# Depthwise taps in sums of 1024, gates on GpSimd and a new order of the half steps in layer 2

## The chip, the cores and the metric

The kernel runs on one core of a Trainium2 chip. A core has TensorE (PE in the profile), VectorE (DVE), ScalarE (ACT), GpSimd (POOL), and SyncE (SP), which here only issues DMAs. Each engine takes its own instructions in order; semaphores hold an instruction until what it needs is there. The metric is the device time of one execution in microseconds, the median of the runs. All data are fp32.

## The reference

Four layers follow each other on x of shape (2, 64, 256, 256), each of the form x + layer(group_norm(x)). Layer 0 is a dilated 3x3 attention, layer 1 two selective scans, layer 3 a blockwise cosine transform with rounding. The change is in layer 2 alone, which is this, cut to what matters:

```python
x = jnp.einsum('bchw,oc->bohw', x, w_in)            # 64 -> 384 channels
xf = jnp.fft.rfft2(patches_8x8(x)) * fft_filter      # one filter per hidden channel
x = unpatch(jnp.fft.irfft2(xf, s=(8, 8)))
x = lax.conv_general_dilated(x, w_dw, padding=[(1, 1), (1, 1)], feature_group_count=384)  # 3x3 depthwise
x1, x2 = jnp.split(x, 2, axis=1)
x = jax.nn.gelu(x1, approximate=False) * x2          # gate x value, 192 channels
return jnp.einsum('bchw,oc->bohw', x, w_out)         # 192 -> 64 channels
```

## The kernel before

Layer 2 goes down the picture in 32 strips of 8 rows. The 384 hidden channels of the two pictures fill six blocks of 128 partitions: a0, a1, a2 are the gates (x1), b0, b1, b2 the values (x2). Blocks 0 and 1 hold 128 channels of one picture each, block 2 the remaining 64 of both.

The work of a strip has a front and a back. The front makes the filtered image of a strip. `norm` (ScalarE) normalizes, `turn` and `fourier` (TensorE, ScalarE) transpose and transform, `hidden` (L915, TensorE) makes the 384 hidden channels in two PSUM tiles `f`, `scaled` (L922, VectorE) multiplies each of the two by the filter into `gf`, `image` (L941, TensorE) transforms back into a PSUM tile `pz`, and ScalarE copies that into the image `z` (L949). There are two `f` tiles and two `pz` tiles in PSUM. Three tiles `z` hold a strip: (a1, a2), (a0, b2), (b1, b0). `edges` (L957, L959, GpSimd) copies the last two rows of a strip to the head of the next and clears the side columns.

The back computes the 3x3 depthwise convolution as nine taps a block, for the strip that the front has finished, in two halves of four rows (1024 elements a partition):

- Values: VectorE, one multiply (L978) and eight multiply-adds (L981) into a PSUM tile `acc`, each on two rows (512 elements), so the two row pairs of a half take turns. Then VectorE multiplies the sum by the gate (L1039, `value_dve`). For b2 of the first half, `value_late` writes the sum to SBUF and GpSimd multiplies (L1047).
- Gates a1 and a2: ScalarE multiplies by the tap (L1016, into one of three `prod` buffers), GpSimd adds (L1020, `gate_pool`); ScalarE applies the gelu (L994) when `flush` is called, three operations into the next sum or in half step 14.
- Gate a0: TensorE multiplies by a diagonal matrix nine times into the PSUM tile `pcv` (L1062, `gate_pe`), and ScalarE applies the gelu from there (L1070).

`project` (L1091, L1098, TensorE) contracts the gated values `gl` of two rows to the output channels, and `finish` (L1109, L1110, VectorE) adds the input, takes statistics for the next normalization, and stores. The PSUM tile `po2`, which transposition, Fourier transform and projection share, has one buffer.

The order is written out by hand. The loop over `u` makes eight steps a strip, each with two half steps (`g`), so a strip has 16 half steps `i`; the back runs nine steps behind the front. `quota(n, i, parts)` deals a list of n operations evenly over the half steps. In each half step, in the program's order: TensorE's `hidden`; up to four of VectorE's taps (`soon`); the two filter products; a projection or output where due; then four places `n`, each with an image, one of TensorE's tap steps, and ScalarE's and GpSimd's share; then the rest of VectorE's taps. TensorE's 36 tap steps go four to a half step, so they fill the first nine; the operations of `gate_pool` fill fourteen. GpSimd's b2 gate is in half step 5; `flush` and `edges` are in half step 14.

VectorE's list of a strip is b2 (late), b0, b1 in the first half and b0, b2, b1 in the second; GpSimd's is a2, a1, a2, a1. A `gl` tile of 1024 elements is drawn from seven buffers, six for the gated blocks and one for the late value.

Of the kernel before, what the change touches and what calls it, by code (L numbers as in the profile page):

```python
# [120 lines left out]
class Kernel:  # L121
# [695 lines left out]
    def layer2(self, x, y, coeffs):  # L817
        nc, tc, a = self.nc, self.tc, self.a
# [14 lines left out]
        nstrip = H // 8  # L833
        with ExitStack() as ctx:
# [5 lines left out]
            with tc.tile_pool(name="l2w", bufs=1) as pool, tc.tile_pool(  # L840
                name="l2wp", bufs=1, space=PSUM
# [5 lines left out]
            taps = {}  # L847
# [17 lines left out]
            pool = ctx.enter_context(tc.tile_pool(name="l2", bufs=2))  # L865
# [1 line left out]
            p_f = ctx.enter_context(tc.tile_pool(name="l2pf", bufs=2, space=PSUM))  # L867
            p_z = ctx.enter_context(tc.tile_pool(name="l2pz", bufs=2, space=PSUM))
            p_c = ctx.enter_context(tc.tile_pool(name="l2pc", bufs=1, space=PSUM))
            p_a = ctx.enter_context(tc.tile_pool(name="l2pa", bufs=2, space=PSUM))  # L870
            p_o = ctx.enter_context(tc.tile_pool(name="l2po", bufs=1, space=PSUM))

            x_half, x_T, x_f, gf, z, gl, xres = {}, {}, {}, {}, {}, {}, {}
# [42 lines left out]
                    ph.append(p)  # L916
                return ph

            def scaled(t, g, ph):
                for b in range(2):  # L920
                    o = pool.tile([P, 2 * HID], F32, name="gf", bufs=8)
                    nc.vector.tensor_tensor(o, feff, ph[b], ALU.mult)  # L922
                    gf[t, g, b] = o
# [45 lines left out]
            def taps_of(s, name, m0, r, last):  # L969


                acc, ops = {}, []

                def step(k, m, n):
                    w, src = taps[name][:, k : k + 1], near(s, name, m0 + m, n, k)
                    if k == 0:
                        acc[m] = p_a.tile([P, 2, W], F32, name="acc")[:, :n]
                        nc.vector.tensor_scalar(acc[m], src, w, None, ALU.mult)  # L978
                        return
                    out = last(m, n) if k == 8 and last else acc[m]  # L980
                    nc.vector.scalar_tensor_tensor(out, src, w, acc[m], ALU.mult, ALU.add)  # L981

                for k in range(9):
                    for m in range(0, r, 2):
                        ops.append(lambda k=k, m=m: step(k, m, min(2, r - m)))
                return ops, acc

            def new_gl(s, h, i, r):
                t = pool.tile([P, 4, W], F32, name="gl", bufs=7)
                gl[s, h, i] = t  # L990
                return t[:, :r]

            def gelu(t):
                nc.scalar.activation(t, t, AF.Gelu)  # L994
# [31 lines left out]
                        out.append(lambda m=m, k=k: step(m, min(2, r - m), k))  # L1026
                return out

            def gate_dve(s, h, i, r):
                t = new_gl(s, h, i, r)  # L1030
                ops, _ = taps_of(s, f"a{i}", 4 * h, r, lambda m, n: t[:, m : m + n])
                return ops + [lambda: gelu(t)]

            def value_dve(s, h, i, r=4):
                ops, acc = taps_of(s, f"b{i}", 4 * h, r, None)

                def gate(m, n):
                    t = gl[s, h, i][:, m : m + n]
                    nc.vector.tensor_tensor(t, t, acc[m], ALU.mult)  # L1039

                return ops + [lambda m=m: gate(m, min(2, r - m)) for m in range(0, r, 2)]

            def value_late(s, h, i):

                t = pool.tile([P, 4, W], F32, name="gl", bufs=7)
                ops, _ = taps_of(s, f"b{i}", 4 * h, 4, lambda m, n: t[:, m : m + n])
                return ops, lambda: nc.gpsimd.tensor_tensor(  # L1047
                    gl[s, h, i], gl[s, h, i], t, ALU.mult
                )

            def gate_pe(s, h, i, r=4):
# [62 lines left out]
            def quota(n, i, parts):  # L1114
                return n * (i + 1) // parts - n * i // parts

            E = mybir.EngineType
            with tc.manual_schedule(engines={E.PE, E.DVE, E.Activation, E.Pool, E.SP}):
# [9 lines left out]
                for u in range(n_u + 12):  # L1128
# [2 lines left out]
                    v = u - 9  # L1131
                    s, j = divmod(v, 8)
                    if j == 0 and 0 <= s < nstrip:
                        dve, gate_late = value_late(s, 0, 2)
                        for h, i in ((0, 0), (0, 1), (1, 0), (1, 2), (1, 1)):
                            dve += value_dve(s, h, i)
                        pe = gate_pe(s, 0, 0) + gate_pe(s, 1, 0)
                        gps = []
                        for h, i in ((0, 2), (0, 1), (1, 2), (1, 1)):
                            gps += gate_pool(s, h, i)  # L1140
                        n_dve, n_gps = len(dve), len(gps)
                    if front:
                        if u % 4 == 2 and u // 4 + 2 < 2 * nstrip:
# [14 lines left out]
                    for g in range(2):  # L1158
                        i = 2 * j + g
                        left = quota(n_dve, i, 16) if 0 <= v and dve else 0  # L1160
                        if front:
                            ph = hidden(t, 2 * odd + g)
                        soon = min(4, left)
                        for _ in range(soon):
                            dve.pop(0)()
                        if front:
                            scaled(t, 2 * odd + g, ph)
                        if out and g == 1 and not odd:
                            finish(*out, po)
                        if out and g == odd:  # L1170
                            po = project(*out)
                        images = ((0, 1), (2,))[g] if 0 < u <= n_u else ()
                        n_pe = min(4, len(pe))
                        if i == 5 and 0 <= s < nstrip:
                            gate_late()
                        for n in range(4):
                            if n < len(images):
                                image(u - 1, images[n])
                            if n < n_pe:
# [139 lines left out]
```

## Time and profile before

| What | us |
|---|---|
| median of 3 runs (lowest, highest) | 19522.35 (19519.64, 19525.44) |
| profiled execution | 19522.79, span 19521.0 |
| layer 2, from its first input to its last output | 15734 to 19197 |
| 31 strips with input, first vector tap to last | 15798 to 19072, 3274 in all |
| busy in these 3274: PE, DVE, ACT, POOL | 2944.9, 3014.1, 2265.7, 2690.5 |

A row of the page's groups reads: line, engine, operation, output <- inputs, shapes, count; behind the bar the time busy in us and the mean of one in ns; then the idle time of that engine just before the group's instructions, and what ended it. A row of a timeline has the start in us, the length, the engine and line, the operation, and in brackets the wait just before it. Two instructions of one engine can overlap by their fill and drain, so the distance between starts says more than the length. The mean granted clock of TensorE is 0.92 of full speed in the 3274 us.

### The profile page before, as it was taken

How to read it: one execution, taken by the hardware profiler on the slowest of the kernel's cores; microseconds unless marked ns; L12 is line 12 of the kernel's file. 1: busy time of each engine (PE TensorE's matmuls, PEld its weight loads, DVE VectorE, ACT ScalarE, POOL GpSimd, SP SyncE). 2: the span in 40 equal slices, each digit the busy share in tenths (PEclk: the TensorE clock that was granted, in tenths of full speed). 3: DMA queues.
4: the chain of work that ended last, by engine and by line, in shares of the span. 5: the costliest groups of instructions: out<-in, count | busy, mean ns of one | idle time of the engine just before them, and what ended most of it. 6: DMA issues, size and time to landing. Idle time of an engine off the chain costs nothing. (4 is left out here: it accounts for less than half of the span.)

```text
span 19521.0 us, 166010 instructions
## 1 busy us (share of the span) xinstructions
PE 14578.1 (75%) x48720; PEld 4850.7 (25%) x48720; DVE 18176.5 (93%) x17790; ACT 12176.5 (62%) x17418; POOL 16771.1 (86%) x8614
## 2 busy tenths in 40 slices
PE   7996767777767777677677677676777689899896
PEld 3441111111111111111111111111111145545454
DVE  6888999999999999999999999999999979999997
ACT  2225666666666666666666666666666656666664
POOL 5997888888888888888888888888888868888885
PEclk9996666666666666666666666666666689999998
DMA  3116666666666666666666666666666611000104
GB/s 122 56 51 151 151 156 148 155 150 151 155 148 155 152 151 153 149 156 153 150 151 151 156 152 151 151 151 157 150 154 150 149 34 32 30 30 30 32 29 146
DMA packets 662208, 2439.06 MB, mean 125 GB/s; under 512 B 131888, under 2 KB 201264, under 8 KB 450160
## 3 DMA queue, kind: packets, MB, share of 16 engines
q1 hardware_dynamic: 661296, 2428.43, 51.9%
q8 instruction: 385, 6.31, 0.1%
q14 instruction: 527, 4.32, 0.1%
HBM read 1990.14 MB, written 437.78 MB: 124 GB/s over the span
## 5 line engine op out<-in xcount | busy, mean ns | idle before, releaser
L792 DVE TENSOR_TENSOR_SCAN h<-da,st,h 128x512 f32<-128x512 f32 x8192 | 9837.5, 1262 | 310.6 <-ACT da L789 226.0
L796 POOL TENSOR_TENSOR h<-h,cb 128x2048 f32<-128x2048 f32 x2048 | 9252.4, 4518 | 164.8 <-DMA d_dv<-du 0.2
L789 ACT ACTIVATE da<-dl,p_a 128x512 f32<-128x512 f32 x8192 | 5564.1, 688 | 3976.2 <-DVE h L792 3884.0
L561 PE MATMUL py<-h,t_c_quad 128*32 128x512 f32 x16384 | 3252.2, 817 | 1646.5 <-POOL h L796 1645.6
L561 PE MATMUL pb<-bc,t_c_sel 64*128 64x512 f32 x3072 | 2697.0, 972 | 2385.8 <-DVE h L773 2380.4
L773 DVE TENSOR_TENSOR h<-dv,pb 128x2048 f32<-128x2048 f32 x1536 | 3470.8, 2260 | 41.0 <-DMA dv<-d_dv 41.0
L1020 POOL TENSOR_TENSOR gl<-gl,prod 128x512 f32<-128x512 f32 x2056 | 2606.7, 1271 | 658.5 <-ACT prod L1016 545.2
L755 POOL TENSOR_TENSOR h<-dv,cb 128x2048 f32<-128x2048 f32 x512 | 2318.7, 4529 | 16.7 <-DMA dl<-d_dl 16.7
L981 DVE SCALAR_TENSOR_TENSOR acc<-z,tap_b,acc 128x512 f32<-128x512 f32 (+1 forms) x3032 | 2046.7, 746 | 1.0
L561 PEld LDWEIGHTS pb<-bc,t_c_sel 64*128 64x128 f32 x3072 | 661.7, 267 | 4411.3 <-DVE h L773 4347.8
L795 POOL COPY st<-h 128x4 f32<-128x4 f32 x2048 | 383.7, 187 | 1362.9 <-DVE h L792 1331.9
L1016 ACT ACTIVATE prod<-z,tap_a 128x512 f32<-128x512 f32 x2056 | 1410.4, 715 | 194.8 <-POOL gl L1020 190.5
L561 PEld LDWEIGHTS py<-h,t_c_quad 128*32 128x32 f32 x16384 | 423.5, 122 | 3812.4 <-POOL h L796 3221.0
L561 PE MATMUL mm<-xin,p_conv 64*128 64x512 f32 x4096 | 1318.5, 773 | 15.7 <-DMA x1t<-y 15.7
L1062 PE MATMUL pcv<-z,diag 128*128 128x512 f32 x2322 | 1142.9, 616 | 44.7 <-ACT gl L1070 41.4
L941 PE MATMUL pz<-t_c_inv,gf 128*128 128x128 f32 (+1 forms) x8192 | 1013.4, 304 | 5.7 <-ACT z L949 4.3
L941 PEld LDWEIGHTS pz<-t_c_inv,gf 128*128 128x128 f32 (+1 forms) x8192 | 822.7, 177 | 488.4 <-issue 310.8
L561 PE MATMUL mm<-u,p_dt 128*128 128x512 f32 x1024 | 929.1, 1061 | 0.0
L561 PE MATMUL py<-u,p_d 128*128 128x512 f32 x1024 | 820.9, 894 | 0.0
L949 ACT COPY z<-pz 128x512 f32<-128x512 f32 x768 | 453.1, 594 | 548.7 <-PE pz L941 494.3
L922 DVE TENSOR_TENSOR gf<-feff,f 128x384 f32<-128x384 f32 x1024 | 518.1, 547 | 218.7 <-PE f L915 218.7
L561 PEld LDWEIGHTS mm<-xin,p_conv 64*128 64x128 f32 x4096 | 459.7, 244 | 981.2 <-issue 981.1
(169 smaller groups left out, 17321.9 us busy)
## 6 DMA issues: line engine op xcount, KB each, us to landing
cb<-d_bc SPq DMA_DIRECT2D x2048, 320.0 KB
dl<-d_dl SPq DMA_DIRECT2D x2048, 256.0 KB
dv<-d_dv SPq DMA_DIRECT2D x2048, 256.0 KB
d_dl<-delta SPq DMA_DIRECT2D x256, 512.0 KB
d_dv<-du SPq DMA_DIRECT2D x256, 512.0 KB
xin<-in_x SPq DMA_DIRECT2D x16, 2048.0 KB
xt<-in_x SPq DMA_DIRECT2D x32, 1024.0 KB
y<-yt SPq DMA_DIRECT2D x128, 256.0 KB
```

The lines of the kernel that those rows point to most:

```text
L561: nc.tensor.matmul(out, lhsT, rhs, start=start, stop=stop)
L755: nc.gpsimd.tensor_tensor(h, t["dv", b], t["cb", b][:, 0].unsqueeze(1).to_broadcast([P, 4, T]), ALU.mult,)
L773: nc.vector.tensor_tensor(h, t["dv", b], pb.unsqueeze(1).to_broadcast([P, 4, T]), ALU.mult)
L789: nc.scalar.activation(da, t["dl", b][:, k], AF.Exp, scale=ws[m]["a"][:, k, j : j + 1])
L792: nc.vector.tensor_tensor_scan(h[:, k], da, h[:, k], state[m, b][:, j, k : k + 1], ALU.mult, ALU.add)
L796: nc.gpsimd.tensor_tensor(h, h, t["cb", b][:, 1 + j].unsqueeze(1).to_broadcast([P, 4, T]), ALU.mult)
L922: nc.vector.tensor_tensor(o, feff, ph[b], ALU.mult)
L941: nc.tensor.matmul(pz[i * n : (i + 1) * n, k, :, 16 * g : 16 * g + 16], gf[t, 2 * e + g, b][:, c0 : c0 + n], inv, start=True, stop=True,)
L981: nc.vector.scalar_tensor_tensor(out, src, w, acc[m], ALU.mult, ALU.add)
L1016: nc.scalar.activation(prod, near(s, name, 4 * h + m, n, k), AF.Copy, scale=w)
L1020: nc.gpsimd.tensor_add(acc, acc, prod)
L1062: nc.tensor.matmul(box["t"], diag[:, k], near(s, f"a{i}", 4 * h + m, n, k), start=k == 0, stop=k == 8,)
```

## The change

1. *Taps of 1024 in one sum.* `taps_of` works on all four rows of a half at once, in a PSUM tile `acc` of 1024 elements with one buffer (before: two of 512). The gates of `value_dve` take 1024 elements, too.
2. *Order of the values.* VectorE's list is b2 (late), b1, b0 in both halves; GpSimd's is a1, a2 in both. GpSimd multiplies b2 in both halves, in half step 8 and in half step 14, the latter between `flush` and `edges`. The value has its own SBUF tile `value` with one buffer, and `gl` six.
3. *TensorE's taps.* `quota` deals the 36 steps over fourteen half steps, two or three in each.
4. *Filter pairs apart.* Two taps stand before the first filter product, and one is put between the two products.

```diff
-            p_a = ctx.enter_context(tc.tile_pool(name="l2pa", bufs=2, space=PSUM))
+            p_a = ctx.enter_context(tc.tile_pool(name="l2pa", bufs=1, space=PSUM))
...
-            def scaled(t, g, ph):
+            def scaled(t, g, ph, between):
                 for b in range(2):
+                    if b:
+                        between()
                     o = pool.tile([P, 2 * HID], F32, name="gf", bufs=8)
                     nc.vector.tensor_tensor(o, feff, ph[b], ALU.mult)
                     gf[t, g, b] = o
...
+            def taps_of(eng, s, name, m0, r, first, last):
+                box = {}
+                def step(k):
+                    w = taps[name][:, k : k + 1]
                     if k == 0:
+                        box["t"] = first()
+                        eng.tensor_scalar(box["t"], near(s, name, m0, r, 0), w, None, ALU.mult)
                         return
+                    out = last(box["t"]) if k == 8 else box["t"]
+                    eng.scalar_tensor_tensor(
+                        out, near(s, name, m0, r, k), w, box["t"], ALU.mult, ALU.add
+                    )
+                return [lambda k=k: step(k) for k in range(9)], box
...
+            def new_acc(r):
+                return p_a.tile([P, 4, W], F32, name="acc")[:, :r]
...
             def value_late(s, h, i):
-                t = pool.tile([P, 4, W], F32, name="gl", bufs=7)
-                ops, _ = taps_of(s, f"b{i}", 4 * h, 4, lambda m, n: t[:, m : m + n])
+                box = {}
+                def last(_):
+                    box["v"] = pool.tile([P, 4, W], F32, name="value", bufs=1)
+                    return box["v"]
+                ops, _ = taps_of(nc.vector, s, f"b{i}", 4 * h, 4, lambda: new_acc(4), last)
                 return ops, lambda: nc.gpsimd.tensor_tensor(
-                    gl[s, h, i], gl[s, h, i], t, ALU.mult
+                    gl[s, h, i], gl[s, h, i], box["v"], ALU.mult
                 )
...
-                        dve, gate_late = value_late(s, 0, 2)
-                        for h, i in ((0, 0), (0, 1), (1, 0), (1, 2), (1, 1)):
-                            dve += value_dve(s, h, i)
+                        dve, gps, gates = [], [], []
+                        for h in range(2):
+                            ops, late_gate = value_late(s, h, 2)
+                            gates.append(late_gate)
+                            dve += ops + value_dve(s, h, 1) + value_dve(s, h, 0)
+                            gps += gate_pool(s, h, 1) + gate_pool(s, h, 2)
                         pe = gate_pe(s, 0, 0) + gate_pe(s, 1, 0)
-                        gps = []
-                        for h, i in ((0, 2), (0, 1), (1, 2), (1, 1)):
-                            gps += gate_pool(s, h, i)
...
-                        soon = min(4, left)
+                        soon = min(2, left)
                         for _ in range(soon):
                             dve.pop(0)()
                         if front:
-                            scaled(t, 2 * odd + g, ph)
+                            more = left > soon
+                            scaled(t, 2 * odd + g, ph, lambda: dve.pop(0)() if more else None)
+                            soon += more
...
-                        n_pe = min(4, len(pe))
-                        if i == 5 and 0 <= s < nstrip:
-                            gate_late()
+                        taps_pe = quota(n_pe, i, 14) if i < 14 and 0 <= v and pe else 0
+                        if i == 8 and 0 <= s < nstrip:
+                            gates.pop(0)()
...
                         if i == 14:
                             flush()
                             if 0 <= s < nstrip:
+                                gates.pop(0)()
                                 if s + 1 == nstrip:
                                     frame(nstrip)
                                 edges(s + 1)
```

More of the change, by code (lines that the diff above doesn't have):

```diff
@@ L967, in near @@
                 return z[s, p][:, e, m0 + dy : m0 + dy + r, dx : dx + W]
[L969 to L975, printed above, removed]
+            def taps_of(eng, s, name, m0, r, first, last):
+                box = {}
+                def step(k):
+                    w = taps[name][:, k : k + 1]
                     if k == 0:
-                        acc[m] = p_a.tile([P, 2, W], F32, name="acc")[:, :n]
-                        nc.vector.tensor_scalar(acc[m], src, w, None, ALU.mult)
+                        box["t"] = first()
+                        eng.tensor_scalar(box["t"], near(s, name, m0, r, 0), w, None, ALU.mult)
                         return
[L980 to L986, printed above, removed]
+                    out = last(box["t"]) if k == 8 else box["t"]
[3 more added lines that the diff above has]
+                return [lambda k=k: step(k) for k in range(9)], box
             def new_gl(s, h, i, r):
-                t = pool.tile([P, 4, W], F32, name="gl", bufs=7)
+                t = pool.tile([P, 4, W], F32, name="gl", bufs=6)
                 gl[s, h, i] = t
                 return t[:, :r]
+            def new_acc(r):
+                return p_a.tile([P, 4, W], F32, name="acc")[:, :r]
             def gelu(t):
@@ L1027, in gate_pool, with gate_dve, gate @@
                 return out
[L1029 to L1032, printed above, removed]
-            def value_dve(s, h, i, r=4):
[L1035 to L1041, printed above, removed]
-            def value_late(s, h, i):
-                t = pool.tile([P, 4, W], F32, name="gl", bufs=7)
-                ops, _ = taps_of(s, f"b{i}", 4 * h, 4, lambda m, n: t[:, m : m + n])
+            def gate_dve(s, h, i, r=4):
+                ops, box = taps_of(
+                    nc.vector,
+                    s,
+                    f"a{i}",
+                    4 * h,
+                    r,
+                    lambda: new_acc(r),
+                    lambda t: new_gl(s, h, i, r),
+                )
+                return ops[:8] + [lambda: (ops[8](), gelu(gl[s, h, i][:, :r]))]
+            def value_dve(s, h, i, r=4):
+                ops, box = taps_of(
+                    nc.vector, s, f"b{i}", 4 * h, r, lambda: new_acc(r), lambda t: t
+                )
+                def gate():
+                    t = gl[s, h, i][:, :r]
+                    nc.vector.tensor_tensor(t, t, box["t"], ALU.mult)
+                return ops + [gate]
+            def value_late(s, h, i):
+                box = {}
[3 more added lines that the diff above has]
+                ops, _ = taps_of(nc.vector, s, f"b{i}", 4 * h, 4, lambda: new_acc(4), last)
                 return ops, lambda: nc.gpsimd.tensor_tensor(
-                    gl[s, h, i], gl[s, h, i], t, ALU.mult
+                    gl[s, h, i], gl[s, h, i], box["v"], ALU.mult
                 )
@@ L1133, in layer2 @@
                     if j == 0 and 0 <= s < nstrip:
-                        dve, gate_late = value_late(s, 0, 2)
-                        for h, i in ((0, 0), (0, 1), (1, 0), (1, 2), (1, 1)):
-                            dve += value_dve(s, h, i)
+                        dve, gps, gates = [], [], []
[4 more added lines that the diff above has]
+                            gps += gate_pool(s, h, 1) + gate_pool(s, h, 2)
                         pe = gate_pe(s, 0, 0) + gate_pe(s, 1, 0)
-                        gps = []
-                        for h, i in ((0, 2), (0, 1), (1, 2), (1, 1)):
-                            gps += gate_pool(s, h, i)
+                        n_pe = len(pe)
                         n_dve, n_gps = len(dve), len(gps)
@@ L1178, in layer2 @@
                                 image(u - 1, images[n])
-                            if n < n_pe:
+                            if n < taps_pe:
                                 pe.pop(0)()
```

## The prediction

> **What bounds the kernel now.** I began with the slices of the page, to find layer 2.
>
> ```profile
> PE   7996767777767777677677677676777689899896
> DVE  6888999999999999999999999999999979999997
> POOL 5997888888888888888888888888888868888885
> ```
>
> Layers 0, 1 and 3 are untouched; layer 2 is the stretch from about the 33rd slice to the 39th, where no engine is at 100% and three are near it. The first vector tap starts at 15798 us and the last strip without fresh input at 19072 us: 31 strips in 3274 us, **105.6 us a strip**. Sixteen half steps make a strip, so 6.6 us each.
>
> Next, the groups of 27 strips in the middle (16077 to 18935 us). Idle time stands behind the bar.
>
> ```profile
> L981 DVE SCALAR_TENSOR_TENSOR acc<-z,tap_b,acc 128x512 f32<-128x512 f32 x2539 | 1718.7, 748 | 0.0
> L922 DVE TENSOR_TENSOR gf<-feff,f 128x384 f32<-128x384 f32 x864 | 437.0, 546 | 148.4 <-PE f L915 148.4
> L1039 DVE TENSOR_TENSOR gl<-gl,acc 128x512 f32<-128x512 f32 x270 | 179.2, 680 | 73.2 <-ACT gl L994 63.1 <-ACT gl L1070 10.1
> L1020 POOL TENSOR_TENSOR gl<-gl,prod 128x512 f32<-128x512 f32 x1728 | 2194.7, 1273 | 507.0 <-ACT prod L1016 412.1
> L1047 POOL TENSOR_TENSOR gl<-gl 128x1024 f32<-128x1024 f32 x27 | 64.0, 2371 | 0.0
> ```
>
> VectorE waits (148.4 + 73.2 + 3.7 before the statistics) / 27 = 8.3 us a strip: 5.5 for TensorE's `f`, 2.7 for a gelu. GpSimd waits far more. Durations overlap, so I took start-to-start times from the timelines. VectorE:
>
> ```profile
> 16796.71 4.70 DVE L981 SCALAR_TENSOR_TENSOR acc<-z,tap_b,acc 128x512 f32<-128x512 f32 x7
> 16803.66 1.02 DVE L922 TENSOR_TENSOR gf<-feff,f 128x384 f32<-128x384 f32 x2 [2.25 <-PE f L915]
> ...
> 16808.27 0.69 DVE L1039 TENSOR_TENSOR gl<-gl,acc 128x512 f32<-128x512 f32 x1 [2.34 <-ACT gl L994]
> ...
> 19178.79 4.23 DVE L981 SCALAR_TENSOR_TENSOR acc<-z,tap_b,acc 128x256 f32<-128x256 f32 x8
> ```
>
> Seven taps of 512 in a row start 0.659 us apart (4.61/7), 0.089 less than one lasts. They alternate between two sums. The last line is the end of the layer, one sum alone: (4.23 - 0.49)/7 = 0.534 us apart, 0.044 *more* than the 0.490 that one lasts.
> VectorE's strip: 108 taps x 0.659 = 71.2; 10 gates x 0.595 = 6.0; 32 filter products x 0.465 = 14.9; 4 outputs with statistics x 1.32 = 5.3. Sum 97.3, plus 8.3 waited, gives the 105.6.
>
> GpSimd, at the seam of two strips, and in the last strip, where nothing else holds it:
>
> ```profile
> 16844.19 8.02 POOL L1020 TENSOR_TENSOR gl<-gl,prod 128x512 f32<-128x512 f32 x6 [0.27 <-ACT prod L1016]
> 16852.16 1.04 POOL L957 COPY z<-z 128x1032 f32<-128x1032 f32 x1
> ...
> 16861.28 1.27 POOL L1020 TENSOR_TENSOR gl<-gl,prod 128x512 f32<-128x512 f32 x1 [5.55 <-ACT prod L1016]
> ...
> 19135.28 10.60 POOL L1020 TENSOR_TENSOR gl<-gl,prod 128x512 f32<-128x512 f32 x8 [0.19 <-ACT prod L1016]
> 19146.07 10.60 POOL L1020 TENSOR_TENSOR gl<-gl,prod 128x512 f32<-128x512 f32 x8 [0.19 <-ACT prod L1016]
> ```
>
> Unhindered, eight adds take 10.79 us, so its strip is 8 x 10.79 = 86.3, one gate 2.4 and the three border copies 3.5 (16852.16 to about 16855.7): 92.2, and 13.4 us of avoidable waiting.
>
> Last, TensorE in the chain of waits:
>
> ```profile
> 16865.49 3.44 PE pcv L1062 x8
> 16868.93 0.84 PE f L915 x4
> ```
>
> Where it sets the pace it runs `f` in 0.84, twelve `pz` in 1.03, eight in 1.09, a tap step (two matmuls) in 0.86 to 1.06. Four tap steps in each of the first nine half steps give 6.9 us each (16747.65 to about 16810); later half steps have none and TensorE waits up to 4.7 us. So VectorE sets most of a strip, TensorE the first nine half steps, GpSimd one gate.
>
> **What the Trainium skill says.** *VectorE: DVE Perf Modes*, section on the TRN2 errata: a latency is paid per instruction, once for a large tile. The trace agrees: 256 elements take 490 ns, 512 take 748. The same page, "The DRAIN you can't avoid", says a semaphore between vector operations costs nothing extra; the trace disagrees for a sum that waits for itself (0.534 us apart; at the fixed part of the alternating taps, 256 elements would be 0.40). *TensorE: Matmul & The Clock Gate*, Part 1: the clock halves after an idle window and needs a busy one to recover. It agrees: after 3.7 us of waiting, `f` x4 took 2.11 us at 16742, not 0.84. *PSUM — Partial Sum Buffer*, Specifications: a bank holds 512 fp32, so a sum of 1024 spans two. No run here shows a vector write over two.
>
> **The change, part by part** (us per strip).
>
> *Taps of 1024.* 108 taps become 54. By the slope 258 ns per 256 elements one lasts 748 + 516 = 1264 ns: 1.175 apart if nothing holds it, 1.308 after its own predecessor. 54 x 1.175 = 63.5. Gates: the two of b2 in the second half move to GpSimd, the other eight become four of 1024, 678 + 2 x 257 = 1192 ns, 1.11 apart: 4.4. With 14.9 and 5.3 unchanged: 88.1. In the changed order 26 of the 58 taps and gates follow directly on the one that they wait for: 26 x 0.133 = 3.5. **VectorE 91.6**, 5.7 less. Bounds: no such holds 88.1, all held 95.8. The two-bank write I take at full pace because `h<-dv,pb` reads 2048 PSUM elements in 2260 ns; its other bound is in the last rival.
>
> *Filter pairs apart.* A tap between the two products removes no instruction. It lets TensorE refill the first `f` bank one tap earlier and fills a hold; counted above. From the last product to the next first one there are three taps, about 3.7 us, where there were seven of 0.659, 4.6; `f` (0.84) and a transpose (0.44) still fit.
>
> *TensorE's taps over fourteen half steps.* 36 steps as before, now 2 or 3 in each. A strip: `f` 13.4, `pz` 25.2, taps 36 x 0.95 = 34.2, transposes and Fourier 5.4, projections 4 x 2.07 = 8.3: 86.5, of which 81 in the fourteen, 5.8 each. Slow clock at the start of a strip adds about 3 in total, two seams between tap groups (`pcv` has one bank) 1.5. That is 6.1 against GpSimd's 6.3 below, so most of the 5.5 us waited for `f` goes. Half steps with a projection reach 7 to 8 and will still stall something.
>
> *Gate order.* Block b1 waits for its gelu at half step 5; the gelu is issued at half step 4, and GpSimd now makes this gate first. Before, both fell in half step 7. I take its 2.7 us as gone; half a step of slack is what hides it.
>
> *GpSimd gates both b2.* 2.4 more. The second gate stands behind the last gelu (0.7 with its signal) and ahead of the border copies, so all that needs the borders moves back by 3.1: ScalarE's first copy of the new image, VectorE's first tap, TensorE's first tap. **GpSimd**: 86.3 + 4.8 + 0.7 + 3.5 = **95.3** without any wait, above VectorE's 91.6. It becomes the bound.
>
> *What is late next.* The second copy, of a0 and b2, ends 0.7 + 2.4 + 2.2 = 5.3 us after the last add. TensorE's first tap waits for it in order, and behind that stands the second image (2.1 with the tap when warm, about 3.9 cold), its copy 0.5 and the second product 0.7, which the first new add needs: 8.6 to 10.4 after the last add, while GpSimd is free at 6.6. I take 9.1, 2.5 of waiting, and 1.0 for the heavy half steps: **98.8 us a strip**. ScalarE's copies are in the same chain; its own work (2265.7 us busy in the 31 strips, 73 each) leaves room.
>
> *Buffers.* One `value` buffer: VectorE writes it again in half step 10, GpSimd reads it in 8; if GpSimd fell two half steps behind, the gate's 2.4 us would be exposed. Six `gl` buffers for six uses: freed by the projection of half step 5, refilled from 7. No DMA and no item of SP's queue moves; the loads run at 30 GB/s here.
>
> *Ends.* The last strip is GpSimd's already (94 us); its extra gate replaces a vector gate of 0.7, so +2. The single last row is unchanged.
>
> Sum against the profiled execution, 19522.8 us (span 19521.0; the median of the runs is 19522.35, the same): 31 x (105.6 - 98.8) = 211, less 2: **19313**.
>
> **Rivals.** *GpSimd alone.* The seam is hidden by the lead of the others, TensorE stays warm: 95.3 a strip, 31 x 10.3 - 2 = 317, 19205. For: GpSimd ran without a gap in the last strip. Against: the first tap's wait for the border copy.
>
> *VectorE stays the bound.* Its waits only change their names: 91.6 + 8.3 = 99.9, gain 175, 19347; with every tap held 104.1, gain 44, 19478. For: at 16838 to 16857 it ran without a pause while the others waited. Against: the named waits come from TensorE's crowding and the late gate.
>
> *Slower: the gate is simply added to GpSimd's loop.* If its 13.4 us of waiting stay, the strip is 95.3 + 13.4 = 108.7, 31 x 3.1 = 96 more, 19620. It decides from 10.3 us of waiting (105.6 - 95.3); I forecast 3.5. For: borders later by 3.1 delay three engines at once, and a cold TensorE follows. Against: some 6 us of the waiting fell in TensorE's crowded half steps.
>
> *The two-bank sum is not at full pace.* At half pace a tap takes some 2.25, VectorE 150, the whole about 20,900. The change loses from a mean tap of about 1.5 (1.24 forecast). Nothing in the profile speaks for it.
>
> **How the numbers follow.** GpSimd with a seam 0.48, GpSimd alone 0.14, VectorE bound 0.27 (a tenth of it within 0.2%), added gate 0.09, two-bank 0.02. About 0.2%, 39 us, is what a measurement of this kernel can tell from no change. Faster: 0.48 + 0.14 + 0.24 = 0.86; same 0.04; slower 0.10, part of the added-gate case ending near zero. The likeliest case alone spans 19260 to 19370 (97 to 100.5 a strip). The 8-in-10 range takes in GpSimd alone at 19200 and VectorE with most of its taps held at 19450.
>
> **What would show it.** Strips 97 to 100 us apart; GpSimd's adds waiting under 6 us a strip beyond their own pace, most at the seam, behind ScalarE; taps of 1024 lasting 1.26 to 1.28 us, 1.18 apart across a filter product and 1.31 in a run; `gf <- f` waits below 3 us a strip; the b1 gate's 2.3 us wait for a gelu gone; the chain of waits with more GpSimd. It is wrong if `f` waits stay at 5 us, if TensorE waits long for the border copies, or if a tap lasts over 1.4.

## The result and the profile after

The changed kernel takes **19422.36 us** (median of 6 runs, 19418.88 to 19425.37) beside 19521.46 for the kernel before in the same runs (6 runs, 19517.28 to 19525.44): a ratio of 0.9949, 95% interval 0.9936 to 0.9962. That is 99 us faster, where 209 were forecast. The profiled execution of the changed kernel has a span of 19423.1 us.

The slices of the page, PE, DVE and POOL again:

```profile
PE   7996677767777677676677677767777679999996
...
DVE  6888999999999999999999999999999978888896
...
POOL 5997888888888888888888888888888878888885
```

In layer 2, from the 34th slice to the 39th, PE now reads 9 throughout, where 8 and 9 took turns, and DVE reads 8 in five slices where it read 9; POOL stays at 8. The groups of the middle strips (16077 to 18935 us, now some 28 strips), read as before:

```profile
L982 DVE SCALAR_TENSOR_TENSOR acc<-z,tap_b,acc 128x1024 f32<-128x1024 f32 x1286 | 1650.8, 1284 | 17.8
L924 DVE TENSOR_TENSOR gf<-feff,f 128x384 f32<-128x384 f32 x895 | 489.5, 547 | 225.7 <-PE f L915 223.3
L979 DVE TENSOR_SCALAR acc<-z,tap_b 128x1024 f32<-128x1024 f32 x168 | 215.8, 1285 | 42.7 <-POOL z L961 39.8
L1051 DVE TENSOR_TENSOR gl<-gl,acc 128x1024 f32<-128x1024 f32 x112 | 136.3, 1217 | 5.8
```
```profile
L1023 POOL TENSOR_TENSOR gl<-gl,prod 128x512 f32<-128x512 f32 x1785 | 2266.8, 1274 | 343.2 <-ACT prod L1019 244.3
L1064 POOL TENSOR_TENSOR gl<-gl,value 128x1024 f32<-128x1024 f32 x56 | 132.0, 2358 | 20.7 <-ACT gl L997 20.7
```
```profile
L1079 PE MATMUL pcv<-z,diag 128*128 128x512 f32 x2011 | 1072.0, 640 | 132.1 <-ACT gl L1087 126.4 <-POOL z L959 5.8
```

and the last of them before the change:

```profile
L1062 PE MATMUL pcv<-z,diag 128*128 128x512 f32 x1944 | 959.5, 616 | 25.7 <-ACT gl L1070 25.7
```

Line numbers have moved: L981 to L982, L922 to L924, L1039 to L1051, L1020 to L1023, L1047 to L1064, L1062 to L1079. VectorE's wait for `f` was to go; it grew, from 148.4 / 27 = 5.5 to 223.3 / 28 = 8.0 us a strip. The gate's wait for a gelu is gone (5.8 us in all of 28 strips, in short gaps behind its own sum's last tap). VectorE's first tap of a strip waits for the border copy, 39.8 / 28 = 1.4. GpSimd's adds wait 343.2 us where they waited 507.0. TensorE's wait for ScalarE's gelu of `pcv`, 25.7 / 27 = 1.0 us a strip before, is 126.4 / 28 = 4.5.

Where that wait sits is seen in one strip. TensorE, ScalarE, VectorE and GpSimd around half step 10, from the timelines:

```profile
16786.69 1.13 PE L1079 MATMUL pcv<-z,diag 128*128 128x512 f32 x2
16791.33 2.07 PE L1079 MATMUL pcv<-z,diag 128*128 128x512 f32 x2 [3.51 <-ACT gl L1087]
16793.33 1.65 PE L915 MATMUL f<-t_w_inT,xf 64*128 64x384 f32 x4
16794.91 2.07 PE L943 MATMUL pz<-t_c_inv,gf 128*128 128x128 f32 x8
```
```profile
16787.78 0.72 ACT L1019 ACTIVATE prod<-z,tap_a 128x512 f32<-128x512 f32 x1 [0.22 <-POOL gl L1023]
...
16790.68 0.59 ACT L1087 ACTIVATE gl<-pcv 128x512 f32<-128x512 f32 x1
```
```profile
16786.11 2.61 DVE L982 SCALAR_TENSOR_TENSOR acc<-z,tap_b,acc 128x1024 f32<-128x1024 f32 x2
16795.01 0.55 DVE L924 TENSOR_TENSOR gf<-feff,f 128x384 f32<-128x384 f32 x1 [6.30 <-PE f L915]
```
```profile
16786.47 10.57 POOL L1023 TENSOR_TENSOR gl<-gl,prod 128x512 f32<-128x512 f32 x8 [0.18 <-ACT prod L1019]
16798.90 10.63 POOL L1023 TENSOR_TENSOR gl<-gl,prod 128x512 f32<-128x512 f32 x8 [1.85 <-ACT prod L1019]
```

36 tap steps dealt over fourteen half steps put the 27th step, the last of a group of nine, in the second place of half step 10 and the first step of the next group in the third place. `pcv` has one buffer, so that step waits until ScalarE has taken the gelu of the group before. The group is complete at 16787.82 (16786.69 + 1.13). ScalarE, which works in order, has a product (with 0.22 us of waiting for GpSimd ahead of it, 16787.78), a normalization, two copies and another product in front of the gelu and starts it at 16790.68. TensorE has waited 3.51 us when it is done, and what follows runs at half the clock (the granted clock is 0.50 from 16791.30 to 16795.00): the tap step takes 2.07 us for 1.13, `f` 1.65 for 0.92, eight `pz` 2.07 for 1.16. All that stood in TensorE's queue behind one tap: VectorE waits 6.30 us for its `f` (16795.01), and GpSimd loses 1.85 us although it is the engine with most to do. The chain of waits goes the same way, through ScalarE's gelu to TensorE and on to VectorE:

```profile
16790.30 0.48 ACT z L951
16790.79 0.50 ACT gl L1087
...
16791.33 2.07 PE pcv L1079 x2
16793.40 1.63 PE f L915 x4
16795.03 0.06 DVE gf L924
```

The seam of two strips on GpSimd (the second gate, then the first add after the borders), and eight of its adds in the last strip, which run at their own pace as before:

```profile
16820.08 2.35 POOL L1064 TENSOR_TENSOR gl<-gl,value 128x1024 f32<-128x1024 f32 x1 [0.74 <-ACT gl L997]
...
16829.63 1.27 POOL L1023 TENSOR_TENSOR gl<-gl,prod 128x512 f32<-128x512 f32 x1 [3.69 <-ACT prod L1019]
```
```profile
19043.57 10.58 POOL L1023 TENSOR_TENSOR gl<-gl,prod 128x512 f32<-128x512 f32 x8 [0.18 <-ACT prod L1019]
```

The seams are not alike, and TensorE's clock tells them apart. In the changed kernel the first add waits 2.23 us in 12 of the 28 seams of the window, 3.6 to 3.8 in 8 and 4.4 to 5.7 in 8. A short and a long one:

```profile
16930.41 1.27 POOL L1023 TENSOR_TENSOR gl<-gl,prod 128x512 f32<-128x512 f32 x1 [2.23 <-ACT prod L1019]
...
17239.38 1.26 POOL L1023 TENSOR_TENSOR gl<-gl,prod 128x512 f32<-128x512 f32 x1 [5.66 <-ACT prod L1019]
```

From the last add to the next first one, the busy time of each engine and, as the third number from the right, the granted clock of TensorE, for the seam shown above and these two:

```profile
16819.35:16829.63 10.28, 8.12 (x37) 4.60 (x38) 8.92 (x11) 4.02 (x7) 5.69 (x7) 0.83 0.13 42
16921.58:16930.41 8.83, 6.58 (x37) 3.81 (x38) 7.33 (x9) 4.03 (x7) 5.68 (x7) 1.00 0.14 45
17227.12:17239.38 12.26, 9.64 (x39) 5.43 (x38) 11.44 (x13) 4.02 (x7) 5.69 (x8) 0.72 0.12 36
```

So the seam lasts 8.8 us at the full clock, and up to 12.3 with part of it at half. Before the change, too, two lengths take turns: the 5.55 us of waiting at 16861.28 that the prediction shows is a short one. From 16334 us on every second seam is like this:

```profile
17603.63 1.27 POOL L1020 TENSOR_TENSOR gl<-gl,prod 128x512 f32<-128x512 f32 x1 [9.29 <-ACT prod L1016]
```

The mean granted clock of the whole window is 0.92 before the change and 0.96 after it.

I took GpSimd's first and last add of each strip from its timeline in this window. "Strip" is the distance of two first adds, "inside" from the first add to the end of the last, "seam" from there to the next first add. The lower part says where it waited for a product (gaps over 0.25 us in front of an add; 72 operations over fourteen half steps tell the half step; "seam" takes in half step 0), all in us a strip, over whole strips with input. The kernels are those of the next section.

| | before | changed | four taps in nine half steps | whole groups | pairs together | all three mended |
|---|---|---|---|---|---|---|
| strip | 105.86 | 102.40 | 105.82 | 100.62 | 100.90 | 97.66 |
| inside | 94.82 | 92.29 | 94.63 | 90.31 | 91.26 | 91.86 |
| seam | 11.05 | 10.10 | 11.19 | 10.31 | 9.64 | 5.81 |
| waits at the seam | 8.2 | 4.2 | 5.2 | 4.6 | 3.7 | 0 |
| half step 2 | 3.1 | 0.9 | 3.0 | 0.4 | 0.4 | 2.2 |
| half steps 4 to 9 | 3.0 | 0.5 | 2.8 | 0.5 | 0.5 | 0.5 |
| half steps 11 to 13 | 0 | 2.2 | 0 | 0 | 1.6 | 0.7 |
| second gate, for its gelu | no gate | 0.7 | 0.7 | 0.7 | 0.7 | 0 |

The change wins 3.46 us a strip. GpSimd's waits in half steps 2 to 9 fell from 6.1 to 1.4 and at the seam from 8.2 to 4.2; against this stand 2.4 more for the gate, 0.7 of waiting for the gelu ahead of it, and 2.2 us of new waits in half steps 11 to 13.

### The profile page after: what moved, and what is told of

It reads as the page before. It is cut to its first block, busy times and chain, and to the rows that moved or that the text cites. A ratio compares the mean times of both kernels' runs of the same rounds, so it can differ in the third digit from the quotient of the medians.

```text
span 19423.1 us, 164029 instructions
## 1 busy us (share of the span) xinstructions
PE 14534.9 (75%) x48720; PEld 4763.2 (25%) x48720; DVE 17991.3 (93%) x15870; ACT 12151.6 (63%) x17418; POOL 16845.3 (87%) x8646
## 5 line engine op out<-in xcount | busy, mean ns | idle before, releaser
L1023 POOL TENSOR_TENSOR gl<-gl,prod 128x512 f32<-128x512 f32 x2056 | 2606.1, 1272 | 460.9 <-ACT prod L1019 346.7
L982 DVE SCALAR_TENSOR_TENSOR acc<-z,tap_b,acc 128x1024 f32<-128x1024 f32 (+1 forms) x1496 | 1901.6, 1271 | 22.3
L1079 PE MATMUL pcv<-z,diag 128*128 128x512 f32 x2322 | 1236.4, 642 | 179.9 <-ACT gl L1087 166.0
L943 PE MATMUL pz<-t_c_inv,gf 128*128 128x128 f32 (+1 forms) x8192 | 964.7, 293 | 7.6 <-ACT z L951 7.3
L924 DVE TENSOR_TENSOR gf<-feff,f 128x384 f32<-128x384 f32 x1024 | 558.7, 547 | 299.9 <-PE f L915 297.4
```

Source lines behind the costliest of these rows:

```text
L943: nc.tensor.matmul(pz[i * n : (i + 1) * n, k, :, 16 * g : 16 * g + 16], gf[t, 2 * e + g, b][:, c0 : c0 + n], inv, start=True, stop=True,)
L982: eng.scalar_tensor_tensor(out, near(s, name, m0, r, k), w, box["t"], ALU.mult, ALU.add)
L1023: nc.gpsimd.tensor_add(acc, acc, prod)
L1079: nc.tensor.matmul(box["t"], diag[:, k], near(s, f"a{i}", 4 * h + m, n, k), start=k == 0, stop=k == 8,)
```

## The experiments

The kernel before took 19521.93 to 19527.35 us beside these kernels, so their times are set beside each other and beside 19422.36; as it took 19521.46 beside the changed kernel, a difference from the changed kernel may be up to 6 us larger than written, and one between two experiments up to 6 us off either way. Two theories stood at the start. **A**: the missing gain sits in the tap groups that end within a half step (the wait above). **B**: it sits in the second b2 gate ahead of the border copies, which makes everything of the next strip late.

### What won the 99 us

*TensorE's taps four to a half step again, the rest of the change kept.*

```diff
-                        taps_pe = quota(n_pe, i, 14) if i < 14 and 0 <= v and pe else 0
+                        taps_pe = min(4, len(pe))
```

> The changed kernel with TensorE's tap steps four to a half step in the first nine, as before the change; order of the values, both b2 gates on GpSimd, taps of 1024 and filter pairs apart stay. If the spreading is what won the changed kernel's 99 us, they go: 19490 or more. If the order of the values won them and the spreading gave about as much as its tap group seams cost (some 50 us), it stays near the changed kernel: 19390 to 19450. Slower than 19560 if half steps of 6.9 us on TensorE now also delay GpSimd with its extra gate.

19529.69 us, ratio 1.0003 (0.9994 to 1.0011): the whole gain is gone.

```profile
16768.52 1.27 POOL L1023 TENSOR_TENSOR gl<-gl,prod 128x512 f32<-128x512 f32 x1 [2.63 <-ACT prod L1019]
...
16783.41 5.33 POOL L1023 TENSOR_TENSOR gl<-gl,prod 128x512 f32<-128x512 f32 x4 [1.13 <-ACT prod L1019]
16789.89 3.85 POOL L1023 TENSOR_TENSOR gl<-gl,prod 128x512 f32<-128x512 f32 x3 [1.14 <-ACT prod L1019]
```

GpSimd waits again in half steps 2, 4 and 5 (2.63, 1.13, 1.14 us), much as before the change, and the mean granted clock of the window is 0.93. So the spreading is what the changed kernel needs for its gain. How much of it comes through the clock, which goes up with it, no run separates. It also shows that GpSimd's second gate isn't simply added to the strip: with 3.1 us more to do, the strip is as long as before, because the waits fell by about as much. The spreading alone in the old order of the values wasn't tried: there VectorE multiplies b0 by gate a0 before the spread taps would have made it.

*The kernel before with taps of 1024 in one sum, nothing else.* Its `taps_of`, `gate_dve`, `value_dve` and `value_late` are written as in the changed kernel, in the old order:

```diff
-                nc.vector.scalar_tensor_tensor(out, src, w, acc[m], ALU.mult, ALU.add)
+                eng.scalar_tensor_tensor(
+                    out, near(s, name, m0, r, k), w, box["t"], ALU.mult, ALU.add
+                )
...
-                        soon = min(4, left)
+                        soon = min(2, left)
```

> The kernel before with one part of the change alone: taps of 1024 in one sum, order, gates and TensorE's deal as before. Taps 1.19 apart across other work and 1.32 in a run, so VectorE needs some 95.5 us a strip where it needed 97.3. If VectorE's work bounds the kernel before as it is, 2 us a strip, about 19465. If its waits for TensorE's crowded half steps and for the late gelu just grow by what is won, 19515 or more.

19526.77 us, ratio 1.0002 (0.9994 to 1.0011). Nothing is won; the strip is 105.73. The groups of VectorE show where the saved work went:

```profile
L922 DVE TENSOR_TENSOR gf<-feff,f 128x384 f32<-128x384 f32 x865 | 438.0, 547 | 166.6 <-PE f L915 166.6
...
L1049 DVE TENSOR_TENSOR gl<-gl,acc 128x1024 f32<-128x1024 f32 x135 | 164.6, 1219 | 102.6 <-ACT gl L995 64.4 <-ACT gl L1082 32.2 <-ACT prod L1017 0.5
```

The wait for `f` is 166.6 / 27 = 6.2 us a strip, from 5.5, and the gates wait (64.4 + 32.2) / 27 = 3.6 for gelus, from 2.7. In all VectorE waits 263.7 / 27 = 9.77 us a strip for other engines, 221.6 / 27 = 8.21 before. Without these waits its strip is 105.73 - 9.77 = 96.0 us, from 105.86 - 8.21 = 97.7: the 1.7 us of work that it saves stand in the waits.

*The changed kernel with taps of 512 in two alternating sums*, the reverse of it (two `acc` of 512, four taps ahead of the products, two between them):

```diff
-            p_a = ctx.enter_context(tc.tile_pool(name="l2pa", bufs=1, space=PSUM))
+            p_a = ctx.enter_context(tc.tile_pool(name="l2pa", bufs=2, space=PSUM))
...
+                for k in range(9):
+                    for m in range(0, r, 2):
+                        ops.append(lambda k=k, m=m: step(k, m, min(2, r - m)))
```

> The changed kernel with one part undone: taps of 512 in two alternating sums, all else (order, b2 gates on GpSimd, TensorE's deal, a pair of taps between the two filter products) as changed. VectorE needs some 96 us a strip, 4 more than changed and about GpSimd's 95.3. If the changed kernel is bound by GpSimd and the seams, at most 1 us a strip is lost: up to 19460. If VectorE's arrival at the strip's end counts in full, 3 to 4 us a strip: 19515 to 19550, no gain left over the kernel before.

19422.04 us, ratio 0.9949 (0.9934 to 0.9964), the changed kernel's time. VectorE waits less, for `f` 145.7 / 28 = 5.2 us for 8.0 and for the borders 27.5 / 28 = 1.0 for 1.4, and the strip is the same 102.40: some 3 us more of work on VectorE cost nothing. In both orders the larger taps only exchange work for waiting.

### Where the other 110 us are

*Whole groups (A): groups of nine end with half steps 3, 6, 10 and 13.*

```diff
-                        taps_pe = quota(n_pe, i, 14) if i < 14 and 0 <= v and pe else 0
+                        deal = (3, 2, 2, 2, 3, 3, 3, 3, 2, 2, 2, 3, 3, 3)
+                        taps_pe = deal[i] if i < 14 and 0 <= v and pe else 0
```

> TensorE's 36 tap steps are dealt (3,2,2,2,3,3,3,3,2,2,2,3,3,3), so a group of nine always ends with its half step and no group starts in the middle of one. Theory A (the excess over the forecast comes from TensorE standing at the seam of two groups until ScalarE's gelu, which is queued behind products that GpSimd holds): the wait of the filter product for f, 8.0 us a strip in the changed kernel, falls to about 3, GpSimd's gap of 1.85 us in the second half of a strip goes, and since VectorE no longer arrives late at the end of the strip the gap at the seam of two strips shrinks from 10.8 to about 9: some 3.5 us a strip, about 19315 us. Theory B (the excess is the gate ahead of the border copies alone): VectorE waits less for f, but the strip stays within 0.8 us of 102.4, 19400 us or more.

19376.82 us, ratio 0.9923 (0.9907 to 0.9940): 46 us below the changed kernel, between the 19315 of A and the 19400 of B.

```profile
DVE gf L924 <- PE f L915: 114.3, 126, 2.5
...
DVE acc L979 <- POOL z L961: 61.6, 28, 2.5
...
PE pcv L1079 <- POOL z L959: 24.5, 28, 6.0
...
PE pcv L1079 <- ACT gl L1087: 7.1, 16, 0.7
```

The columns are the total, the number of waits and the longest, in us. TensorE's wait for the gelu fell from 126.4 to 7.1 and VectorE's for `f` from 223.3 to 114.3; GpSimd's gap in half step 11 is gone. A is right about this wait and it is worth 1.8 us a strip. At the same time the waits for the border copies grew, VectorE's from 39.8 to 61.6.

*Borders ahead of the gate (B): in half step 14 the second gate comes behind `edges`.*

```diff
-                                gates.pop(0)()
                                 if s + 1 == nstrip:
                                     frame(nstrip)
                                 edges(s + 1)
+                                gates.pop(0)()
```

> In half step 14 the border copies stand ahead of GpSimd's second b2 gate, so the borders no longer wait for the last gelu and the gate (3.1 us). Theory A (TensorE's seam inside the strip makes VectorE late, and that sets the strip seam): borders come earlier, but TensorE's f of the next strip still waits for VectorE's late product, so at most 0.8 us a strip is won, 19395 us or more. Theory B (the borders set the strip seam): 2 to 3 us a strip, 19330 to 19360 us.

19399.52 us, ratio 0.9935 (0.9920 to 0.9950): 23 us below the changed kernel. The wait for `f` stays (228.3), as A says. A allows for it with 19395 or more, and B's 19330 to 19360 isn't reached: the gate's place costs, and is the smaller part.

*Both.*

```diff
+                        deal = (3, 2, 2, 2, 3, 3, 3, 3, 2, 2, 2, 3, 3, 3)
...
                                 edges(s + 1)
+                                gates.pop(0)()
```

> Both edits. If each theory holds a part, the borders begin to matter once VectorE is in time: more than the sum of the two single gains; GpSimd near its floor of 95 to 97 us a strip, 19200 to 19260 us. If only A holds, as the first kernel, about 19315. If only B holds, as the second.

19342.95 us, ratio 0.9906 (0.9891 to 0.9920): 79 us below, a little more than the two alone (46 + 23), but 83 us short of the 19260 that were to come if each theory holds a part. The strip is 99.47.

*The second b2 gate as VectorE's last operation of a strip, none of it on GpSimd.*

```diff
-                return ops, lambda: nc.gpsimd.tensor_tensor(
+                eng = nc.vector if h else nc.gpsimd
+                return ops, lambda: eng.tensor_tensor(
...
+                            if h:
+                                dve.append(late_gate)
...
-                                gates.pop(0)()
```

> The b2 gate of the second half is VectorE's last operation of the strip instead of GpSimd's; all else as in the changed kernel. If GpSimd's load of 95.3 us a strip is the bound (the forecast's step), it loses the gate and the wait for the last gelu, 3.1 us, and the strip falls by 2 to 3 us, 19330 to 19360 us. If the stall at TensorE's seam sets VectorE's arrival (theory A), VectorE gets 1.2 us more and the strip stays within 1 us of 102.4, or grows: 19390 to 19460 us.

19398.93 us, ratio 0.9935 (0.9921 to 0.9950): as much as the borders ahead of the gate (23 us), and not what 2.4 + 0.7 us less work on GpSimd would be worth (96). GpSimd's adds wait 402.8 us for 343.2. GpSimd's own work alone is thus no bound of the changed kernel. But VectorE got 1.5 us more to do in exchange (a gate of 1484 ns), so what GpSimd's 2.4 us cost by themselves this run doesn't show.

*No tap step in half step 0, then three in each.* That takes TensorE's first wait for the borders out of the seam:

```diff
+                        deal = (0, 3, 3, 3, 3, 3, 3, 3, 3, 3, 3, 2, 2, 2)
+                        taps_pe = deal[i] if i < 14 and 0 <= v and pe else 0
```

> As e1_seam, whole groups of nine, but dealt (0,3,3,3,3,3,3,3,3,3,3,2,2,2): no TensorE tap in half step 0, so the second image of a strip no longer stands behind a tap that waits for the border copy and runs at the slow clock. If that chain sets the seam of two strips (the forecast's step on what is late next), GpSimd's first add comes 1.5 to 2 us earlier than in e1_seam, 45 to 60 us in all, about 19325. If VectorE's own first tap, which waits for the same border copy, sets it, nothing is won: 19365 or more.

19415.27 us, ratio 0.9946 (0.9931 to 0.9961): a miss. It is 38 us above whole groups alone, although the seam fell from 10.31 to 7.63 us. The gaps moved into half steps 1 and 2 (1.6 and 2.9 us; inside rose from 90.31 to 94.40).

```profile
DVE gf L924 <- PE f L915: 157.5, 92, 3.2
...
DVE acc L979 <- POOL z L961: 74.0, 27, 3.0
...
PE pcv L1079 <- ACT gl L1087: 37.4, 28, 1.4
```

VectorE's first tap now waits 74.0 / 27 = 2.7 us for the border copies, 61.6 / 28 = 2.2 with whole groups, and its filter products stand behind that tap.

*The same deal and the borders ahead of the gate.*

```diff
+                        deal = (0, 3, 3, 3, 3, 3, 3, 3, 3, 3, 3, 2, 2, 2)
...
                                 edges(s + 1)
+                                gates.pop(0)()
```

> e5_first with the border copies ahead of the second b2 gate. With the three waits gone the strip should come near GpSimd's own 95 to 97 us: 19230 to 19290 us. If TensorE with three tap steps in ten half steps running becomes the bound instead (its half step is then 6.3 us on average), 19330 or more, with VectorE waiting for f.

19298.13 us, ratio 0.9886 (0.9869 to 0.9902), strip 98.19. With the borders early the same deal that lost 38 us now wins 45 against the other one (19342.95): the seam falls from 9.48 to 7.51. So the deal is worth nothing until the borders come early, and its three tap steps in ten half steps running are not by themselves what made the run before slow. It stays 8 us above the 19290 expected.

*That kernel with the second b2 gate on VectorE.*

```diff
+                eng = nc.vector if h else nc.gpsimd
...
+                        deal = (0, 3, 3, 3, 3, 3, 3, 3, 3, 3, 3, 2, 2, 2)
...
-                                gates.pop(0)()
```

> Whole groups of nine for TensorE, none in half step 0, and the second b2 gate of a strip as VectorE's last operation in place of GpSimd's (2.4 us less on GpSimd, 1.1 to 1.2 us more on VectorE, the borders directly behind the last gelu). If GpSimd's own work sets the strip once the tap groups and the borders are mended (19298), it is 31 x 2.4 = 74 us faster still, 19210 to 19245. If VectorE and TensorE set it as much, the products of the next strip come 1.2 us later and nothing or less is won: 19280 to 19335.

19296.76 us, ratio 0.9883 (0.9868 to 0.9898): within 2 us of the kernel with the gate on GpSimd. The seam fell to 6.65, and the inside rose from 90.68 to 91.73 although GpSimd does the same work in it. So here, too, handing the gate to VectorE buys nothing; what GpSimd would gain if no other engine took it over no run shows.

### Filter pairs

*The changed kernel with the two filter products directly behind each other.*

```diff
-                            more = left > soon
-                            scaled(t, 2 * odd + g, ph, lambda: dve.pop(0)() if more else None)
-                            soon += more
+                            scaled(t, 2 * odd + g, ph, lambda: None)
```

> The changed kernel without the tap between the two filter products: they stand directly behind each other again, taps of 1024 and everything else as in the changed kernel. GpSimd and the seams of the strips set the pace: within 25 us of the changed kernel, 19400 to 19450. If VectorE's own pace sets it, each half step holds one more tap behind its own sum (0.13 us) and the first f tile comes free one tap later: 16 x 0.13 = 2.1 us a strip, 65 us, 19485 or more.

19385.16 us, ratio 0.9927 (0.9911 to 0.9944): 37 us *below* the changed kernel, outside both expectations. Setting the pairs apart costs. What it does to `f` is seen at a seam; TensorE in the changed kernel, and in this one:

```profile
16820.76 0.91 PE L915 MATMUL f<-t_w_inT,xf 64*128 64x384 f32 x2 [1.87 <-DVE gf L924]
16822.42 0.91 PE L915 MATMUL f<-t_w_inT,xf 64*128 64x384 f32 x2 [0.75 <-DVE gf L924]
16823.26 1.55 PE L943 MATMUL pz<-t_c_inv,gf 128*128 128x128 f32 x12
```
```profile
16813.92 1.37 PE L915 MATMUL f<-t_w_inT,xf 64*128 64x384 f32 x4 [2.38 <-DVE gf L924]
16815.22 1.30 PE L943 MATMUL pz<-t_c_inv,gf 128*128 128x128 f32 x12
```

With a tap between the products TensorE can fill the first `f` tile (16820.76) while VectorE is at that tap. But its next instruction needs the second tile, so its queue stands 0.75 us more until VectorE has done the tap and the second product, and `f` ends 3.1 us after VectorE's first product began (16820.16). With the products together all four matmuls run at once, and `f` ends (16815.22, where `pz` begins) 1.9 us after VectorE's first product (16813.32). A strip is 1.5 us shorter, by the table 1.0 of it inside, in half steps 2 and 11 to 13, and 0.5 at the seam. VectorE waits 165.7 us for `f`, not 223.3, and 11.7 for the borders, not 39.8.

That `f` ends earlier is seen; that GpSimd gains by this at the seam is not. In both kernels 12 of the 28 seams run at the full clock, and in these its first add waits the same 2.23 us. What differs are the other seams: 8 of them in the changed kernel, 4 here, have over 5 us at half clock. By which way the 37 us are lost stays open.

*Whole groups with none in half step 0, borders ahead of the gate, pairs together.*

```diff
-                            scaled(t, 2 * odd + g, ph, lambda: dve.pop(0)() if more else None)
+                            scaled(t, 2 * odd + g, ph, lambda: None)
...
+                        deal = (0, 3, 3, 3, 3, 3, 3, 3, 3, 3, 3, 2, 2, 2)
...
                                 edges(s + 1)
+                                gates.pop(0)()
```

> Whole groups of nine, borders ahead of the second b2 gate (19298 with the filter products a tap apart), and the filter products together again. If GpSimd sets the strip: 19280 to 19325. If the handshake of VectorE and TensorE sets it now, the later refill of f shows: 19340 or more, with more waiting of the filter product for f.

**19281.84 us**, ratio 0.9875 (0.9860 to 0.9890), the best version: 141 us below the changed kernel. GpSimd's seam, and its next gaps:

```profile
16783.03 2.36 POOL L1064 TENSOR_TENSOR gl<-gl,value 128x1024 f32<-128x1024 f32 x1
16785.35 10.75 POOL L1023 TENSOR_TENSOR gl<-gl,prod 128x512 f32<-128x512 f32 x8
16797.71 1.27 POOL L1023 TENSOR_TENSOR gl<-gl,prod 128x512 f32<-128x512 f32 x1 [1.62 <-ACT prod L1019]
16800.38 10.65 POOL L1023 TENSOR_TENSOR gl<-gl,prod 128x512 f32<-128x512 f32 x8 [1.40 <-ACT prod L1019]
```

The first add follows on the gate with no wait. What is left is mostly in half step 2, here 1.62 and 1.40 us. The strip is 97.66 against 94.6 of GpSimd's own work (the forecast's 95.3 less the 0.7 of waiting for the gelu). What stands behind the last 3 us wasn't tried and is open.

## Why the prediction was right in sign and wrong in size

It had a strip of 98.8 us; it is 102.4. 2.6 of the 3.6 missing are inside the strip (92.3 measured; the forecast's 95.3 without the second gate, the gelu ahead of it and the borders is 88.7, and it added 1.0 for heavy half steps), the other 1.0 at the seam (10.1 for 9.1).

- *Taps of 1024.* Right: 1284 ns for 1264, 1.19 us to a filter product behind it and 1.32 in a run, no loss from two banks, gates 1217 ns for 1192. VectorE waits (223.3 + 39.8) / 28 = 9.4 us a strip for other engines, so its own work is 102.4 - 9.4 = 93.0, forecast 91.6. The rival in which VectorE stays the bound falls: taps of 512 give it some 3 us more to do, and the time is the same. What the step didn't say is that the larger taps buy nothing; the two runs on them show that.
- *Filter pairs apart.* **Wrong in sign.** "It lets TensorE refill the first `f` bank one tap earlier and fills a hold": both are so, and it costs 37 us all the same. The step left out that TensorE's queue then stops at the second bank (0.75 us at the seam shown), with all that stands behind it; that this is what costs the 37 us is likely, not shown.
- *TensorE's taps over fourteen half steps.* Right as the source of the gain (99 us, all gone without it). **This is the step that failed in size, the largest single part of what is missing**: "two seams between tap groups (`pcv` has one bank) 1.5" measured 4.5, of it 3.5 in half step 10, and the clock was at half after it. It was taken as TensorE's own work and spread over fourteen half steps, 5.8 to 6.1 each; in truth most of it falls into one half step and delays the whole queue there, so VectorE waits 6.3 us and GpSimd 1.85. With it falls "most of the 5.5 us waited for `f` goes", which became 8.0. Whole groups, which take this wait to 7.1 / 28 = 0.3 us, give back 46 of the 110 us.
- *Gate order.* Right as far as seen: the 2.7 us for a gelu are gone. No run changes the order alone.
- *GpSimd gates both b2.* The terms are right: gate 2.36 us, gelu ahead of it 0.74, borders to 6.6 us after the last add. "It becomes the bound" is half right: it has the most to do, and the page's chain holds 4% of GpSimd where it held 2%, but handing the second gate to VectorE gains 23 us and not 96, and in the mended kernel nothing.
- *What is late next.* The chain named is the one seen, and 9.1 us from the last add to the next first one measured 10.1 on average. At the full clock it is 8.8, near the 8.6 that the step had for a warm TensorE; with some 3.4 us at half clock it is 10.3, as its cold figure of 10.4 has it. But 16 of the 28 seams have a stretch at half clock, and 8 of them one long enough for 11 to 12.3 us, which the step didn't have. So the chain was right, and the slow clock was given too little weight.
- *Rivals.* "The gate is simply added" (108.7) did not come: GpSimd waits 102.4 - 95.3 = 7.1 us beyond its own work, under the 10.3 from which it decides. "GpSimd alone" (95.3) wasn't reached by any kernel; the best is 97.66.

With the tap groups, the borders and the pairs mended the kernel is 31 us under the 19313 forecast. That doesn't bear the forecast out: it takes another deal of the taps, and it undoes two things that the change did, the pairs apart and the second gate ahead of the borders.

## What to carry to other kernels

When work of one engine is spread evenly, look at where a tile with one buffer changes hands: put that point at the end of a slot, and price a wait there with everything in the same queue behind it and with the queue of the engine that frees it. An engine that fills two buffers in order can gain nothing from the first coming free early; here the time even fell by 37 us when both came free together. Where one engine's clock follows its own waits, look at more than one strip: the same order gave seams of 8.8 and 12.3 us here. Work saved on an engine that already waits turns into waiting; the two runs on tap size moved VectorE's waits by 1.6 and 3.2 us a strip and the time by none.

## What the runs showed of the hardware

A vector sum over two PSUM banks keeps its pace: 1284 ns for 1024 elements against 748 for 512, close to the 1264 that the slope of the smaller sizes gives; this goes beyond the Trainium skill's *PSUM — Partial Sum Buffer*, Specifications, which gives the size of a bank (512 fp32 values) and no pace for a vector operation over two. A tap that follows directly on its own predecessor starts 1.32 us after it (the median of 502 pairs); from a tap to the filter product behind it, which doesn't wait for it, it is 1.19 (starts at 16795.49 and 16796.68). So each direct dependence costs about 0.13 us.

TensorE's clock was at half after a wait of 3.51 us (the tap step 2.07 us, four `f` 1.65), in agreement with *TensorE: Matmul & The Clock Gate*, Part 1. In this trace so long a wait isn't needed. At the seam shown, waits of 1.87 and 0.75 us for VectorE's products (16820.76, 16822.42) were followed by 3.4 us at half clock from 16824.2; at the next seam waits of 1.74 and 0.75 us were followed by none. In the middle window the granted clock of the changed kernel is either 1.00 or 0.50, and its 43 stretches at half last 3.41 us (13) or 6.83 us (30); all its changes lie on one grid of 3.41 us. So where a wait falls on that grid may matter as much as its length; no run here moves one against the other.
